# First unit of the attention's maxima moved up: half-head stores, tiles taken in pieces, and two row transfers on ScalarE's queue

## The chip, the cores and the metric

The kernel runs on one core of a Trainium2 chip, as one launch. The metric is the time of one execution on the device, in microseconds (us). The median of three runs of the kernel before is 1208.4 us (1208.12 to 1208.51). One more execution was profiled.

The engines are called as the profile calls them: PE (TensorE; PEld is its weight load), DVE (VectorE), ACT (ScalarE), POOL (GpSimd) and SP (SyncE, which here only issues transfers). ACT issues transfers as well, between its own instructions, and each engine takes its instructions in order.

## What is computed

The input is x of 8 batches by 1024 tokens by 256 columns, in float32. The reference applies half a mixture-of-experts layer, an attention layer with 16 heads of 16 columns, and another half mixture-of-experts layer, each on the layer norm of x and each added to x. An expert that more tokens choose than its capacity allows is dropped whole:

```python
x = x + 0.5 * ffn(layernorm(x), gate_w, w1, b1, w2, b2)
x = x + attn(layernorm(x), Wq, bq, Wkv, bkv, Wo, bo)
x = x + 0.5 * ffn(layernorm(x), gate_w, w1, b1, w2, b2)
...
# attn:  q, k, v = heads of 16 columns;  dots = (q * 16**-0.5) @ k.T, masked above the diagonal
#        out = softmax(dots) @ v;  return out @ Wo.T + bo
# ffn:   top-2 of softmax(x @ gate_w.T); keep = counts <= cap; only kept experts add to the output
```

The kernel computes the attention first as if no expert were kept, counts the choices of both gates on the way, and runs the experts only where one is kept. In the profiled execution that does not happen, so all of the time is the function `attention`.

## The kernel before

**Units.** For each batch b the 16 heads are handled as four units of four heads: unit u = 4 b + g, 32 units in all (NU). A unit has 18 maxima steps (M) and 18 exponent steps (E). An M step (`m_steps`, `fill`) multiplies a piece of q by k on PE into the tile sm, adds the causal mask on PE (masked, before_k), and DVE reduces it to row maxima (mx). After the M steps of one half of the queries, `settle` joins and negates the maxima on DVE (mxr, mneg, mside), and `send` stores them to DRAM (rows) and loads them back as rows (neg) for the next product. An E step (`e_steps`, `fill`) adds neg by a product with take_m and the product of k and q into sc on PE; ACT takes the exponential (pT), POOL zeroes the masked part of diagonal pieces, and a few steps later PE multiplies pT by the values (pav).

**Order.** Every instruction of the attention is issued through a `Lane` (lines 618 to 635), which pins each engine's instructions, and each transfer queue, to the source's order; this is why the profile puts nearly everything on L626, and why groups are told apart by tile. The loop over u runs the E steps of unit u in turns with M steps of the next units; PE fills the turns with pieces from `work` (next batch's transposes pta, projections pq, values pv), at `rate` pieces per gap, one gap for every third step, and DVE with steps from `side`.

**Projections.** `project(b, gp)` makes q and k of eight heads (gp is 0 or 1). Each is split on ACT and POOL into a high and a low part (whole, high, low), so that products of two parts keep float32's accuracy. SP stores each part for all eight heads, one transfer of shape 8x16x512 (256 KB) a time, 16 of them per (b, gp), to the DRAM tile parts; `fetch(u)` loads the four heads of a unit into a qk tile by four transfers.

**The start.** Lines 1206 to 1240 are written out by hand: read x of batch 0 (in pieces of two, two and four tiles of 128 tokens) and of batch 1, transpose the weights (`turning`), normalise (`prepare_first`, `normed`), transpose (`enter`), project the first eight heads by halves of the tokens with a `fetch` of unit 0 after each half, all values of batch 0 (`values_of(0)`), then the statistics and the first four normalised tiles of batch 1 (`prepare(1)`), memsets, and the fetch of unit 1. Then comes the loop, with u = -1 first: the 18 M steps of unit 0, in turns with `project(0, 1)` at a gap every second step. After them the first gate's choice (`gate_first(0)`, small DVE operations such as lc_f, key_f, cand_f) and the bias of the residual (`biased_late(0)`, x_a on POOL) are taken as side steps.

Of the kernel before, what the change touches and what calls it, by code (L numbers as in the profile page):

```python
# [10 lines left out]
F32 = mybir.dt.float32  # L11
# [9 lines left out]
P = 128  # L21
# [8 lines left out]
def macaron_kernel(  # L30
# [98 lines left out]
                base=-(64 * h + k), channel_multiplier=1,  # L129
            )  # L130
    take_m = const.tile([P, P], F32R, name="take_m")
    nc.vector.tensor_copy(take_m, rows.to_broadcast([P, P]))

    wqT = const.tile([P, DC, D], F32, name="wqT")
    wkT = const.tile([P, DC, D], F32, name="wkT")
# [466 lines left out]
    def attention(run_no, src, dst, gate0, logits, tally):  # L602
# [4 lines left out]
        with stack:  # L607
# [76 lines left out]
            def normed(b, jj):  # L684
                mv, ve, rstd = lns[b]
                for j in (2 * jj, 2 * jj + 1):
                    xn = xns[b, j] = norm.tile([P, D], F32, tag="xn", name=f"xn_a{b}_{j}", bufs=4)
                    ln_apply(xn, xbs[b], j, mv, rstd[:, j : j + 1])
                    yield
                if b:  # L690
                    biased(b, jj)

            coming = {}
# [28 lines left out]
            def prepare_first():  # L722
                st, mv = ln_tiles("a0", "a")
                ve = norm.tile([P, TB], F32, tag="vea", name="ve_a0")
                rstd = norm.tile([P, TB], F32, tag="rstda", name="rstd_a0")
                lns[0] = (mv, ve, rstd)
                for n in (slice(0, TB // 2), slice(TB // 2, TB)):
                    for j in range(TB)[n]:
                        ln_stats(xbs[0], j, st, mv)
                    on.gpsimd.tensor_scalar(ve[:, n], mv[:, n, 1], EPS, None, ALU.add)  # L730
                    on.gpsimd.tensor_tensor(rstd[:, n], ve[:, n], half[:, n], ALU.pow)

            def enter(b):
                xnT = xnTs[b] = ap.tile([P, DC, S], F32, tag="xnT", name=f"xnT{b}", bufs=1)
# [19 lines left out]
                    yield True  # L754


            def project(b, gp):
                xnT = xnTs[b]
                parts = parts_d[b, gp] = passing.tile([2, 8, 4, HD, S], F32, tag=f"parts{gp}", name=f"parts{b}_{gp}")
                for s0 in range(0, S, 512):  # L760
                    for t, (wT, bT, scale) in enumerate(((wqT, bqT, QSCALE), (wkT, bkT, 1.0))):
                        pq = bank(f"pq{b}_{gp}_{s0}_{t}")
                        for o in (0, 256):
                            for c in range(DC):
                                product(
                                    pq[:, o : o + 256],
                                    wT[:, c, gp * P : (gp + 1) * P],
                                    xnT[:, c, s0 + o : s0 + o + 256],
                                    start=(c == 0),
                                    stop=(c == DC - 1),  # L770
                                )
# [3 lines left out]
                        high = ap.tile([P, 512], F32R, tag="high", name=f"high{b}_{gp}_{s0}_{t}", bufs=3)  # L775
                        low = ap.tile([P, 512], F32R, tag="low", name=f"low{b}_{gp}_{s0}_{t}", bufs=3)
                        on.scalar.activation(whole, pq, AF.Identity, bias=bT[:, gp : gp + 1], scale=scale)
                        on.scalar.copy(high, whole)
                        on.gpsimd.tensor_tensor(low.bitcast(F32), whole, high.bitcast(F32), ALU.subtract)
                        for c in range(4):  # L780
                            part = (high, low)[c // 2 if t else c % 2]
                            on.sync.dma_start(out=parts[t, :, c, :, s0 : s0 + 512], in_=part.bitcast(F32))
                        yield True


# [62 lines left out]
            def m_steps(u):  # L848
# [56 lines left out]
                def settle(hf):  # L905
                    mx = ap.tile([P, 4, 2, 2], F32, tag="mxr", name=f"mxr{u}_{hf}")
                    on.vector.tensor_reduce(
                        mx.rearrange("p x b a -> p x a b"),
                        mx_tiles[u % 3][hf].rearrange("p h r (a b) s -> p (h r) a b s", a=2),
                        AX.X,  # L910
                        ALU.max,
                    )
                    yield
                    mx = mx.rearrange("p x b a -> p x (b a)")
                    neg = ap.tile([P, 4, 2, 4], F32R, tag="mneg", name=f"mneg{u}_{hf}")
                    high, low = neg[:, :, 0], neg[:, :, 1]
                    on.vector.tensor_scalar(high, mx, -1.0, None, ALU.mult)
                    yield
                    on.vector.scalar_tensor_tensor(
                        low.bitcast(F32), mx, -1.0, high.bitcast(F32), ALU.mult, ALU.subtract  # L920
                    )
                    yield
                    turned = ap.tile([P, 32], F32, tag="mside", name=f"mside{u}_{hf}")
                    on.vector.transpose(turned, neg.bitcast(F32).rearrange("p x c i -> p (x c i)"))
                    start(send(hf, turned), 0)
                    yield

                def send(hf, turned):
                    rows = passing.tile([8, 512], F32, tag="rows", name=f"rows{u}_{hf}")
                    on.sync.dma_start(out=rows.rearrange("c (i s q) -> s c i q", i=4, s=4), in_=turned)  # L930
                    yield 6
                    for h in range(2):
                        on.sync.dma_start(
                            out=negs[u % 2][hf][64 * h : 64 * h + 2, :, :512].bitcast(F32),
                            in_=rows[4 * h : 4 * h + 4].rearrange("(r c) s -> c r s", c=2),
                        )
# [271 lines left out]
            next(turning, None)  # L1208
            next(turning, None)
            drain(read(1))  # L1210
            for t in (vaugs[0], *mx_tiles[0]):
                on.gpsimd.memset(t, 1.0 if t is vaugs[0] else -3.0e38)
            prepare_first()
            for jj in range(2):
                drain(normed(0, jj))
            next(turning, None)
            entering = enter(0)
            next(entering)
            next(entering)
            for jj in range(2, 4):  # L1220
                drain(normed(0, jj))
            projecting = project(0, 0)
            for _ in range(8):
                next(projecting)
            drain(fetch(0, 0, 512))
            drain(entering)
            drain(projecting)
            drain(fetch(0, 512, 512))
            drain(turning)
            drain(values_of(0))  # L1230
            drain(prepare(1))
            for t in (vaugs[1], *mx_tiles[1], *mx_tiles[2]):
                on.gpsimd.memset(t, 1.0 if t is vaugs[1] else -3.0e38)
            for pair_of in negs:
                for t in pair_of:
                    on.gpsimd.memset(t.bitcast(F32), 0.0)
            drain(fetch(1))

            work = deque([project(0, 1)])
            side += [biased_late(0), gate_first(0)]  # L1240
            timed = []
            behind = [0.0]
            last_on = []
# [41 lines left out]
            def maxima():  # L1285
                v, k = divmod(stream[0], 18)
                if v == NU:
                    return
                if k == 0:
                    units[v] = m_steps(v)  # L1290
                steps, settle, done = units[v]
                steps[k]()
                if k == max(done, 8) or k == 17:
                    side.appendleft(settle(int(k == 17)))
                    urgent[0] = 4
                if k == 17:
                    units.pop(v)
                stream[0] += 1

            for u in range(-1, NU):  # L1300
                b, g = divmod(u, NG)
                rate, every = 17 / 12, FILLS
                if u < 0:
                    pass
                elif g == 0:
                    spare[0] = False
                    if b + 1 < B:
# [1 line left out]
                        if b:  # L1309
                            work.append(mixed(leave(b - 1), project(b + 1, 1)))  # L1310
                        else:
                            work.append(project(b + 1, 1))
                        work.append(values_of(b + 1))
                    if b:
                        start(divide(b - 1, 1, 0), 4)
                        after[u - 1, 1] = divide(b - 1, 1, 1)
                        side.append(gate_first(b))
                elif g == 1 and b + 1 == B:
                    work.append(leave(b - 1))
                elif g == 2:  # L1320
                    if b == 0:
                        start(read(2), 40)
# [14 lines left out]
                    start(fetch(u + 2, lag=6), 8)  # L1337
                if u < 0:
                    for n in range(18):
                        step(maxima, 2, 4 if n < 5 else 4 / 3, 1)  # L1340
                else:
                    if u == 0:
                        for n in range(3):
# [86 lines left out]
```

## Time and profile before

| what | us |
|---|---|
| median of three runs | 1208.4 |
| the profiled execution's own time | 1207.5 |
| its span, first to last instruction | 1205.5 |
| busy: PE, DVE, ACT, POOL | 1138.4, 935.2, 735.6, 433.8 |
| first M reduction on DVE starts | 46.16 |
| first exponential (unit 0) starts on ACT | 77.35 |
| first exponential of unit 4, the second batch's first | 220.2 |

Times inside the profile are counted from the first instruction. The page cuts the span in 40 slices of 30 us. A row of a timeline has its start, its length, the engine, the operation, output<-input, shapes and a count, and in brackets the idle time before it and what ended it; a "q" behind an engine means the part of it that issues transfers. In the view by stretches each engine's busy time is followed by its number of instructions, and at the end stand the granted PE clock, the busy share of the 16 DMA engines and the GB/s they moved.

### The profile page before, as it was taken

To read this page: it belongs to the slowest core of one execution; us is meant where nothing else is said; L and a number is where in the kernel's file an instruction comes from. 1 tells how busy PE (TensorE), PEld (TensorE's weight loads), DVE (VectorE), ACT (ScalarE), POOL (GpSimd) and SP (SyncE) were. 2 spreads that over 40 slices of the span, in tenths; PEclk is the share of its full clock that TensorE was granted. 3 is DMA by queue.
4 is the path that set the end of the run, shared out by engine and by line. 5 is a ranking of instruction groups with operands and counts; after the bars stand their busy time and mean duration, and the time that the engine had idled before them with its cause. 6 is when DMAs were issued, how large, how long until landed. Compare 5 with 4: busy or idle time off the path is not lost.

```text
span 1205.5 us, 36314 instructions
## 1 busy us (share of the span) xinstructions
PE 1138.4 (94%) x15178; PEld 663.1 (55%) x15178; DVE 935.2 (78%) x1652; ACT 735.6 (61%) x955; POOL 433.8 (36%) x772
## 2 busy tenths in 40 slices
PE   6789899999999999999999999999999999999983
PEld 4445555655556555655556555565556555555542
DVE  2687558887788877988788877888789888798834
ACT  3236656766666666665666656566666666665671
POOL 4633313543333423532235433333235322232331
PEclk9879999999999999999999999999999999999997
DMA  5644654354554646455563645546564555543211
GB/s 178 222 168 141 209 173 128 111 196 153 171 185 154 198 159 190 143 172 177 157 201 113 207 153 168 169 155 202 160 181 150 176 174 177 155 136 109 63 42 39
DMA packets 108517, 190.25 MB, mean 158 GB/s; under 512 B 24752, under 2 KB 42296, under 8 KB 108344
## 3 DMA queue, kind: packets, MB, share of 16 engines
q1 hardware_dynamic: 104952, 185.59, 47.8%
q8 instruction: 122, 2.00, 0.7%
q10 hardware_dynamic: 3392, 2.24, 0.6%
q14 instruction: 51, 0.42, 0.1%
HBM read 94.50 MB, written 93.31 MB: 156 GB/s over the span
## 4 chain that ended last, share of the span: by engine, by line
PE 76%; DVE 13%; DMA 5%; issue 1%; ACT 1%; POOL 1%; SPq 1%; POOLq 0%; ACTq 0%; DVEq 0%
PE sc L626 22%; PE pav L626 21%; PE sm L626 15%; PE pq L626 8%; DVE mx L626 8%; PE px L626 4%; PE pv L626 4%; PE pta L626 2%; DVE st_a L626 1%; DMA few<-sums 1%; DMA neg<-rows 1%; DMA rows<-mside 1%; SPq L626 1%; DVE mv_a L626 1%; DMA qk<-parts 1%
## 5 line engine op out<-in xcount | busy, mean ns | idle before, releaser
L626 DVE TENSOR_REDUCE mx<-sm 128x2 f32<-128x1024 f32 (+2 forms) x576 | 684.7, 1215 | 161.6 <-PE sm L626 159.9
L626 ACT ACTIVATE pT<-sc 128x1024 f32<-128x1024 f32 x576 | 573.0, 1022 | 309.6 <-PE sc L626 297.9
L626 PE MATMUL pav<-pT,vaug 128*32 128x256 f32 (+3 forms) x4608 | 329.7, 387 | 2.0 <-ACT att L626 1.4
L626 POOL TENSOR_SCALAR_AFFINE_SELECT pT<-pT 128x256 f32<-128x256 f32 (+1 forms) x448 | 191.0, 443 | 297.2 <-ACT pT L626 290.4
L626 PE MATMUL sm<-qk 64*128 64x512 f32 (+3 forms) x1536 | 266.2, 384 | 17.4 <-DVE mx L626 8.4
L626 PE MATMUL sc<-neg,take_m 64*128 64x512 f32 x1152 | 263.7, 454 | 16.6 <-DVE mx L626 8.9
L626 PE MATMUL sc<-qk 64*128 64x512 f32 (+3 forms) x1536 | 228.7, 334 | 0.0
L626 PEld LDWEIGHTS sm<-qk 64*128 64x128 f32 x1536 | 140.7, 187 | 120.4 <-issue 51.9
L626 POOL TENSOR_TENSOR low<-whole,high 128x512 f32<-128x512 f32 x64 | 82.0, 1282 | 311.3 <-ACT high L626 302.5
L626 PEld LDWEIGHTS pav<-pT,vaug 128*32 128x32 f32 x4608 | 113.7, 109 | 108.0 <-issue 52.2
L626 PEld LDWEIGHTS sc<-neg,take_m 64*128 64x128 f32 x1152 | 109.4, 186 | 106.8 <-issue 53.6
L626 PEld LDWEIGHTS sc<-qk 64*128 64x128 f32 x1536 | 146.2, 186 | 16.3
L626 PE MATMUL sm<-masked,before_k 64*128 64x128 bf16 (+1 forms) x1280 | 86.3, 213 | 0.0
L626 PE MATMUL pq<-xnT,wqT 128*32 128x256 f32 x1024 | 76.3, 391 | 0.5 <-ACT xnT L626 0.5
L626 PE MATMUL px<-woT,on 128*32 128x264 f32 x1024 | 76.5, 387 | 0.2 <-ACT on L626 0.2
L626 PE MATMUL pq<-xnT,wkT 128*32 128x256 f32 x1024 | 73.2, 395 | 0.0
L626 PE MATMUL pv<-wvT,xnT 128*32 128x264 f32 x1024 | 72.3, 390 | 0.0
L626 PEld LDWEIGHTS <-before_k 64*128 64x128 bf16 x1280 | 37.9, 96 | 43.1 <-issue 26.6
L626 POOL TENSOR_TENSOR x_a<-x_a,bo_all 128x512 f32<-128x512 f32 x32 | 41.6, 1304 | 28.1 <-DVE xn_a L626 28.1
L626 PEld LDWEIGHTS pq<-xnT,wqT 128*32 128x32 f32 x1024 | 34.0, 112 | 31.8 <-issue 13.9
L626 DVE TENSOR_TENSOR x_a<-px,x_a 128x256 f32<-128x256 f32 x64 | 26.2, 410 | 31.2 <-PE px L626 30.6
L626 PEld LDWEIGHTS px<-woT,on 128*32 128x32 f32 x1024 | 34.7, 110 | 26.6 <-issue 9.8
(131 smaller groups left out, 741.4 us busy)
## 6 DMA issues: line engine op xcount, KB each, us to landing
qk<-parts SPq DMA_DIRECT2D x124, 512.0 KB
parts<-high SPq DMA_DIRECT2D x128, 256.0 KB
parts<-low SPq DMA_DIRECT2D x128, 256.0 KB
sums<-att SPq DMA_DIRECT2D x62, 256.0 KB
out_dram<-x_a SPq DMA_DIRECT2D x16, 512.0 KB
on<-sums SPq DMA_DIRECT2D x30, 256.0 KB
rs<-inv SPq DMA_DIRECT2D x30, 256.0 KB
x_a<-in_L_attn_x_dram SPq DMA_DIRECT2D x13, 512.0 KB
```

The lines of the kernel that those rows point to most:

```text
L626: i = call(*args, **kwargs)
```

## The change

The start is rearranged, and some rules of the first units change with it:

- The tile take_m is made later on DVE, inside `prepare_first`, which now takes statistics of tiles 0 to 1, 2 to 3, then normalises these four, and only then takes the statistics of tiles 4 to 7. POOL's memsets of the first vaug and mx tiles move from before the first rstd operations to between them.
- The first projection stores only the first four heads of each part (transfers of 4x16x512, 128 KB) and keeps the other four heads' stores in a list `later`. Its parts live in buffers of the tag pT (six of them) and no longer in high and low (three each).
- After the second half's fetch of unit 0, the 16 stores of `later` are issued, then the fetch of unit 1, then the statistics of batch 1 and the memsets. The values of batch 0 go from the hand-written start into `work`, ahead of `project(0, 1)`. The M steps of unit 0 have a gap after every step (16/5 pieces for five steps, then 16/13). The first four normalised tiles of batch 1 become side steps.
- Unit 0's maxima of the first half are settled after its fifth M step and no longer after the ninth. Unit 0's row transfers (rows, neg) are issued by ACT and no longer by SP.
- The first gate's choice and the bias of batches 0 and 1 move into the loop's units 0 and 1. In batch 0 the rate is 13/12 pieces a gap, before 17/12, and batch 1's second projection is mixed with its values where before it preceded them.

```diff
@@ prepare_first
-                for n in (slice(0, TB // 2), slice(TB // 2, TB)):
-                    for j in range(TB)[n]:
+                def some(j0, j1):
+                    for j in range(j0, j1):
                         ln_stats(xbs[0], j, st, mv)
...
+                some(0, 2)
+                some(2, 4)
+                drain(normed(0, 0))
+                next(turning, None)
+                drain(normed(0, 1))
+                on.vector.tensor_copy(take_m, rows.to_broadcast([P, P]))
+                on.gpsimd.memset(vaugs[0], 1.0)
+                for t in mx_tiles[0]:
+                    on.gpsimd.memset(t, -3.0e38)
+                some(4, 8)
@@ project
+                first = b == gp == 0
...
+                        if first:
+                            both = ap.tile([P, 2, 512], F32, tag="pT", name=f"split{s0}_{t}", bufs=6)
+                            high, low = both[:, 0].bitcast(F32R), both[:, 1].bitcast(F32R)
...
                             part = (high, low)[c // 2 if t else c % 2]
-                            on.sync.dma_start(out=parts[t, :, c, :, s0 : s0 + 512], in_=part.bitcast(F32))
+                            heads = parts[t, :, c, :, s0 : s0 + 512]
+                            if first:
+                                later.append((heads[4:], part[P // 2 :]))
+                                heads, part = heads[:4], part[: P // 2]
+                            on.sync.dma_start(out=heads, in_=part.bitcast(F32))
@@ settle and send of m_steps
-                    start(send(hf, turned), 0)
+                    start(send(hf, turned), 0 if u else 2)
...
+                    queue = on.sync if u else on.scalar
...
-                    yield 6
+                    yield 6 if u else 4
@@ the hand-written start
-            for t in (vaugs[0], *mx_tiles[0]):
-                on.gpsimd.memset(t, 1.0 if t is vaugs[0] else -3.0e38)
             prepare_first()
-            for jj in range(2):
-                drain(normed(0, jj))
-            next(turning, None)
             entering = enter(0)
...
             drain(fetch(0, 512, 512))
+            for heads, part in later:
+                on.sync.dma_start(out=heads, in_=part.bitcast(F32))
+            drain(fetch(1))
+            preparing = prepare(1)
+            for _ in range(TB + 1):
+                next(preparing)
...
             drain(turning)
-            drain(values_of(0))
-            drain(prepare(1))
...
-            drain(fetch(1))
-            work = deque([project(0, 1)])
-            side += [biased_late(0), gate_first(0)]
+            work = deque([values_of(0), project(0, 1)])
+            side.append(preparing)
@@ the loop
-                if k == max(done, 8) or k == 17:
+                if k == (max(done, 8) if v else done) or k == 17:
...
-                rate, every = 17 / 12, FILLS
+                rate, every = (17 if b else 13) / 12, FILLS
...
-                            work.append(project(b + 1, 1))
-                        work.append(values_of(b + 1))
+                            work.append(mixed(values_of(b + 1), project(b + 1, 1)))
+                        if b:
+                            work.append(values_of(b + 1))
...
-                        step(maxima, 2, 4 if n < 5 else 4 / 3, 1)
+                        step(maxima, 1, 16 / 5 if n < 5 else 16 / 13, 1)
```

In the built program the order of transfers on SP becomes: eight half stores, four loads of unit 0, eight half stores, four loads of unit 0, the 16 half stores of `later`, four loads of unit 1 (512 KB each), the 16 full stores of `project(0, 1)`, and then the first two loads of unit 2. ACT's order is, around its own transfers: rows of unit 0's first half, whole and high of the next part, neg (two transfers), three more pairs of whole and high, rows of the second half, xnT, the first pT, a small exponential of the gate, neg (two transfers), the second pT.

More of the change, by code (lines that the diff above doesn't have):

```diff
@@ L131, in macaron_kernel @@
     take_m = const.tile([P, P], F32R, name="take_m")
-    nc.vector.tensor_copy(take_m, rows.to_broadcast([P, P]))
     wqT = const.tile([P, DC, D], F32, name="wqT")
@@ L689, in normed @@
                     yield
-                if b:
+                if b > 1:
                     biased(b, jj)
@@ L726, in prepare_first @@
                 lns[0] = (mv, ve, rstd)
-                for n in (slice(0, TB // 2), slice(TB // 2, TB)):
-                    for j in range(TB)[n]:
+                def some(j0, j1):
+                    for j in range(j0, j1):
                         ln_stats(xbs[0], j, st, mv)
+                    n = slice(j0, j1)
                     on.gpsimd.tensor_scalar(ve[:, n], mv[:, n, 1], EPS, None, ALU.add)
                     on.gpsimd.tensor_tensor(rstd[:, n], ve[:, n], half[:, n], ALU.pow)
+                some(0, 2)
[8 more added lines that the diff above has]
+                some(4, 8)
             def enter(b):
@@ L754, in enter @@
                     yield True
+            later = []
             def project(b, gp):
+                first = b == gp == 0
                 xnT = xnTs[b]
@@ L774, in project @@
                         whole = ap.tile([P, 512], F32, tag="whole", name=f"whole{b}_{gp}_{s0}_{t}")
-                        high = ap.tile([P, 512], F32R, tag="high", name=f"high{b}_{gp}_{s0}_{t}", bufs=3)
-                        low = ap.tile([P, 512], F32R, tag="low", name=f"low{b}_{gp}_{s0}_{t}", bufs=3)
+                        if first:
+                            both = ap.tile([P, 2, 512], F32, tag="pT", name=f"split{s0}_{t}", bufs=6)
+                            high, low = both[:, 0].bitcast(F32R), both[:, 1].bitcast(F32R)
+                        else:
+                            high = ap.tile([P, 512], F32R, tag="high", name=f"high{b}_{gp}_{s0}_{t}", bufs=3)
+                            low = ap.tile([P, 512], F32R, tag="low", name=f"low{b}_{gp}_{s0}_{t}", bufs=3)
                         on.scalar.activation(whole, pq, AF.Identity, bias=bT[:, gp : gp + 1], scale=scale)
@@ L924, in settle @@
                     on.vector.transpose(turned, neg.bitcast(F32).rearrange("p x c i -> p (x c i)"))
-                    start(send(hf, turned), 0)
+                    start(send(hf, turned), 0 if u else 2)
                     yield
                 def send(hf, turned):
+                    queue = on.sync if u else on.scalar
                     rows = passing.tile([8, 512], F32, tag="rows", name=f"rows{u}_{hf}")
-                    on.sync.dma_start(out=rows.rearrange("c (i s q) -> s c i q", i=4, s=4), in_=turned)
-                    yield 6
+                    queue.dma_start(out=rows.rearrange("c (i s q) -> s c i q", i=4, s=4), in_=turned)
+                    yield 6 if u else 4
                     for h in range(2):
-                        on.sync.dma_start(
+                        queue.dma_start(
                             out=negs[u % 2][hf][64 * h : 64 * h + 2, :, :512].bitcast(F32),
@@ L1219, in attention @@
             next(entering)
-            for jj in range(2, 4):
-                drain(normed(0, jj))
             projecting = project(0, 0)
@@ L1225, in attention @@
             drain(fetch(0, 0, 512))
+            for jj in range(2, 4):
+                drain(normed(0, jj))
             drain(entering)
@@ L1228, in attention @@
             drain(fetch(0, 512, 512))
-            drain(turning)
-            drain(values_of(0))
-            drain(prepare(1))
[L1232 to L1236, printed above, removed]
-            drain(fetch(1))
-            work = deque([project(0, 1)])
-            side += [biased_late(0), gate_first(0)]
+            for heads, part in later:
[4 more added lines that the diff above has]
+                next(preparing)
+            for k in range(2):
+                for t in negs[k]:
+                    on.gpsimd.memset(t.bitcast(F32), 0.0)
+                for t in mx_tiles[k + 1]:
+                    on.gpsimd.memset(t, -3.0e38)
+            on.gpsimd.memset(vaugs[1], 1.0)
+            drain(turning)
+            work = deque([values_of(0), project(0, 1)])
+            side.append(preparing)
             timed = []
@@ L1316, in attention @@
                         after[u - 1, 1] = divide(b - 1, 1, 1)
-                        side.append(gate_first(b))
+                    side.append(gate_first(b))
+                    if not b:
+                        side.append(biased_late(b))
                 elif g == 1 and b + 1 == B:
                     work.append(leave(b - 1))
+                elif g == 1 and b == 0:
+                    side.append(biased_late(1))
                 elif g == 2:
```

## The prediction

> **What bounds the kernel now.** I read the 40 slices first, then the view by stretches (one stretch a unit), then the chain in order of time for the first 140 us, then SP's timeline.
>
> ```profile
> PE   6789899999999999999999999999999999999983
> PEclk9879999999999999999999999999999999999997
> ```
>
> PE is full from the fourth slice on. Only the first 90 us and a place in the fifth slice have room, so the change, which leaves batch 1 and later alone, can win or lose only before unit 4.
>
> ```profile
> 77.30:115.20 37.90, 37.34 (x497) 22.63 (x496) 27.38 (x41) 23.67 (x28) 12.14 (x20) 0.91 0.43 143
> 115.20:156.00 40.80, 35.05 (x456) 20.38 (x452) 22.82 (x26) 23.67 (x28) 12.52 (x22) 0.92 0.60 194
> 156.00:190.10 34.10, 34.10 (x456) 20.02 (x454) 22.73 (x26) 23.50 (x39) 7.85 (x17) 0.99 0.40 132
> 190.10:220.20 30.10, 27.53 (x318) 15.35 (x316) 27.57 (x48) 19.23 (x20) 11.44 (x24) 1.00 0.44 141
> ```
>
> These are units 0 to 3, from first exponential to first exponential. Unit 1 has 5.75 us of idle PE, unit 3, which has no filler left, 2.57.
>
> ```profile
> 42.22 1.68 POOL rstd_a L626
> 43.92 2.33 DVE xn_a L626 x4
> 46.24 1.14 DVE mx L626
> ...
> 67.08 0.92 SPq L626
> 68.09 0.81 SPq L626
> 68.95 1.03 SPq L626
> 70.03 1.22 SPq L626
> 71.36 4.99 DMA neg<-rows
> 76.49 0.84 PE sc L626 x4
> 77.35 1.03 ACT pT L626
> ```
>
> The first reductions wait behind batch 1's normalised tiles on DVE (46.24), and the first exponential behind the rows, which stand on SP's queue behind stores of parts (67.08 to 76.49). Both waits are what the change removes. Next, what SP's queue carries:
>
> ```profile
> 26.84 6.48 SPq L626 DMA_DIRECT2D qk<-parts  x4
> 42.95 9.33 SPq L626 DMA_DIRECT2D qk<-parts  x8
> 143.28 1.19 SPq L626 DMA_DIRECT2D qk<-parts  x1
> ```
> ```profile
> 152.87 0.80 PE L626 MATMUL sm<-qk 64*128 64x512 f32 x2 [5.75 <-issue]
> ```
> ```profile
> 54.00:57.00 3.00, 1.09 (x12) 0.37 (x4) 3.00 (x4) 0.26 (x1) 3.00 (x4) 1.00 1.00 401
> 62.00:66.00 4.00, 2.48 (x16) 0.94 (x16) 4.00 (x6) 0.47 (x1) 1.27 (x1) 0.50 0.53 190
> ```
>
> From 54 to 57 only loads of qk run: all 16 DMA engines busy, 401 GB/s. From 62 to 66 only stores of parts: share 0.53, 190 GB/s, so 262 KB take 1.38 us. In the trace's semaphore updates (my source for every landing below) a load of 128x512 raises its semaphore 16 times, a store of 8x16x512 nine times, rows (4x32x32) five times, neg (2x2x512) three times: one more than the outermost count. So a store uses eight engines. The loads of 26.84 and 42.95 landed by 36.9 and 53.7, the one of 143.28 at 152.78; the last is unit 1's stall.
>
> **The change, part by part.**
>
> *Half stores.* A first-half store is 4x16x512. Not in this trace; the ends are half of 1.38 (0.69 us, still eight engines) and the whole 1.38 (four engines). I take 1.38: the rows transfer, outermost count four, shows four engine updates. Weighed against a rule: the Trainium skill, "DMA: Bandwidth & Descriptors", section "Why a DMA increments its semaphore by 16 and not by 1", says that a transfer of these queues runs on the largest number of engines up to 16 that divides the slowest dimension of both sides, on the lowest-numbered ones. That speaks against this change: four heads mean four engines, and half the bytes take the same time. By the rule the sum is the one below, by halved stores that of the first rival.
>
> *The transfer chain.* ACT can copy xnT at 11.45, when its own transfers are issued (10.39 + 1.04), not 11.86: everything is 0.4 earlier. The first 16 stores and eight loads then take as long as before, so unit 0's second half lands at 53.7 - 0.4 = 53.3. Then come 16 more stores, which before did not exist: 16 x 1.38 = 22.1, to 75.4. Three of unit 1's four loads wait for them. Before, the second load landed 3.0 after the last store (48.8 to 51.8); 512 KB in place of 256 KB adds 0.65, and the next two follow by 1.25 (57.1, 58.4, 59.6 before): 79.0, 80.3, 81.5. Before, unit 1's loads were in at 59.6.
>
> *The maxima.* Unit 0's M steps start when its first loads are in (34.5, before 46.16), but the sixth needs the second half and waits until 48.6 to 52.4; twelve more at 1.2 to 1.5 us end at 67 to 71, before 72.9. That gain is worth nothing by itself: PE's order has unit 1's first three sm (81.5 + 0.8) and a pta (1.1 to 1.9) in front of the first sc.
>
> *ACT in order.* The fourth high of `project(0, 1)` takes the first one's buffer (three buffers) and waits for its second store, the third on SP behind unit 1's loads: 81.5 + 3 x 1.38 = 85.6. Then high 0.6, the issue of rows 0.5, xnT 0.6: first exponential at 87.4, before 77.35. The second stands on ACT behind two neg transfers. These wait for the rows and for the sixth store, whose semaphore one of them shares (81.5 + 6 x 1.38 = 89.8). Rows in SP's queue took 4.94 (66.08 to 71.02), on an idle one 1.96 (92.48 to 94.44). On ACT's own queue, beside stores, they take something between: 88.8 to 91.8. With 0.5 for the issues the second starts at 90.3 to 92.3, before 79.7. Here a rule bears too: the same page, "Issuing engines are not separate DMA queues", says that transfers of ACT and SP interleave on the same 16 engines, so that another issuer saves only issue time. By it the end is 4.9 and not 2.0; since the sixth store holds the issue until 89.8 anyway, that moves the second exponential by 1.5 at most.
>
> PE used part of that wait for pta, which before stood between second and third exponential (3.4 us apart), so the lag shrinks from 11.6: third about 92.9 (83.1), fourth 95.4 (86.1). **First stage: +9 us** (8 to 10.5).
>
> *Units 0 to 3.* PE's work up to unit 4 is the same, so its idle time decides. (a) Unit 1's stall. Before: rows issued at 131.62 with four stores right ahead of them; SP waited for them until 139.27 (7.65), issued four stores (4.0) and the load, which landed 9.5 later: 21.2 in all, needed after 15.4. In the new order two loads stand ahead of the rows: 2.0 to 4.9, say 3.5, then 4.0 and 9.5 make 17.0, needed after 14.5 (13 pieces a unit make it 33 us, not 35). 2 to 2.5 of 5.75 stay: -3.5. (b) The clock was at half from 149.6 to 156.4, with 3.5 us of PE work in it: -1.5 if the shorter stall leaves the clock alone, -0 if not; -1. (c) With filler in unit 3 its 2.57 idle goes: -2.6. (d) The gate's some two dozen DVE operations fall into unit 0, the bias (1.3 us each on POOL) into units 0 and 1. DVE is busy 27.4 of unit 0's 37.9 and POOL 12.1, so both are covered; uncovered, DVE's reductions (1.2 us) set the unit's pace: 0 to +1, say 0.5. (e) The stores of batch 1's second projection spread into units 2 and 3, beside their loads; batches 1 to 7 show idle PE before sm of 0.3 to 1.0 in such places: +0.5.
>
> The take_m copy (0.2), statistics in smaller pieces and the moved memsets cost nothing: xnT waits for ACT's own transfers at 11.45, stats of tiles 4 to 7 end near 13, and their four xn (1.4) are done by 16, while PE reaches them at 17.7. Uncovered, they cost their own 1 to 2 us.
>
> **Sum:** 9 - 3.5 - 1 - 2.6 + 0.5 + 0.5 = +2.9. Against the profiled execution: 1207.5 (span 1205.5 and 2.0 around it) becomes 1210.4; the median lies 0.9 higher, so **1211.3**, 0.24% slower. A measurement of this kernel tells about 0.2% (2.4 us) from no change.
>
> **Rivals.**
> 1. *Half stores take half the time (0.69).* The first eight end about 6 earlier, the second eight 5.5 more, and the 16 late ones take 11: unit 1's loads land at 59. Then M sets the pace: start at 31 (PE's pt_b ends), five steps with eight pv of 0.89 until 42.6, thirteen of 1.2 to 1.5: 58 to 62; first exponential near 65, -11 to -12 for the stage, with units 0 to 3 at -6: **1191**. For it: it is what half the bytes suggest. Against: the counts of updates.
> 2. *Not slower: the loop makes up for the start.* Stores of 1.3 (the spacing of the first eight landings), rows in 2.0, and unit 1's stall gone with its clock loss: +7 - 5.75 - 1.75 - 2.6 = -3: **1205**. For it: the lower rate leaves SP fewer stores around unit 3's loads. It decides when the last of them lands before the unit's last M step.
> 3. *The stall stays in unit 1, whole.* The new order still has four stores right before that load. If SP is held by neg as long as before, (a) and (b) are lost, and one more such wait in units 2 or 3 costs 1 to 2: **1216.5**.
>
> **How the numbers follow.** Forecast 0.42, with its own range 1208 to 1214: slower 0.22, same 0.20. Rival 1: 0.12, faster. Rival 2: 0.22, faster 0.15, same 0.07. Rival 3: 0.24, slower 0.23, same 0.01. Together faster 0.27, same 0.28, slower 0.45. The range 1196 to 1219 holds the forecast, rival 2 and most of rival 3, and leaves out rival 1 and the tail of 3.
>
> **What would show it.** Right: stores of 4x16x512 with five updates and a DMA share near 0.27 from 54 to 75; unit 1's loads landing near 81; PE idle for some ten us before sm<-qk there; first exponential near 87, unit 4's near 223; an idle piece of 2 us before sm<-qk in unit 1. Wrong: a first exponential before 75 (rival 1), unit 4 before 218 (rival 2) or after 226 (rival 3). What I may have missed is a wait in units 0 to 3 that the new order makes, and the clock, which was at half for 6.8 us pieces in the old start and whose pieces I can't place in the new one.

## The result

| | kernel before | changed kernel |
|---|---|---|
| median of six runs of each on one chip | 1207.25 us | 1216.31 us |
| the profiled execution's own time (span) | 1207.5 (1205.5) | 1216.3 (1214.6) |
| first exponential | 77.35 | 86.56 |
| start of units 1, 2, 3 and 4 | 115.2, 156.0, 190.1, 220.2 | 127.5, 163.7, 195.6, 228.7 |
| start of unit 31 | 1150.9 | 1158.0 |

The ratio is 1.0076, with a 95% interval of 1.0059 to 1.0093: the change makes the kernel slower by 0.76%, 9.1 us. The prediction said slower by 0.24%, so the sign is right and the forecast size is a third of the real one. The time lies above the forecast's own range of 1208 to 1214 us.

Two rows of the slices of the changed kernel answer to those shown of before:

```profile
PE   6758999999999999999999999999999999999983
PEclk9778999999999999999999999999999999999997
```

The head has become thinner: the third slice (61 to 91 us) was 8 and is 5. The view by stretches, from first exponential to first exponential of units 0 to 3:

```profile
86.60:127.50 40.90, 34.48 (x456) 20.77 (x452) 29.11 (x48) 22.57 (x29) 12.43 (x21) 0.91 0.49 162
127.50:163.70 36.20, 33.95 (x422) 19.13 (x420) 23.51 (x27) 22.14 (x29) 17.20 (x26) 1.00 0.50 160
163.70:195.60 31.90, 31.90 (x422) 18.61 (x420) 22.74 (x26) 22.87 (x33) 9.07 (x18) 1.00 0.47 148
195.60:228.70 33.10, 32.76 (x420) 18.57 (x420) 28.33 (x49) 22.35 (x29) 12.07 (x21) 1.00 0.56 184
```

PE is idle in them for 6.42, 2.25, 0 and 0.34 us (length less busy time); before it was 0.56, 5.75, 0 and 2.57. Unit 1's idle time has shrunk and unit 3's is nearly gone, as forecast, but unit 0 has 5.9 us of new idle time, as much as both gave. Unit 4 starts 8.5 later than before, where 2.9 was forecast. Batch 1 takes 139.5 us in both, and the rest differs by 0.7, so in these two profiles the loss is made before unit 4.

Where it is made, in the timelines of the changed kernel, first PE, then ACT:

```profile
77.78 0.79 PE L625 MATMUL sm<-qk 64*128 64x512 f32 x2 [10.16 <-DMA qk<-parts]
95.27 1.93 PE L625 MATMUL pta<-ident,xn_a 128*32 128x128 f32 x32 [4.66 <-ACT xnT L625]
```
```profile
85.42 0.62 ACT L625 CAST high<-whole 128x512 fp32r<-128x512 f32 x1 [16.99 <-DMA parts<-high]
85.50 0.54 ACTq L625 DMA_DIRECT2D rows<-mside  x1
...
86.56 1.03 ACT L625 ACTIVATE pT<-sc 128x1024 f32<-128x1024 f32 x1
...
93.13 0.55 ACTq L625 DMA_DIRECT2D neg<-rows  x2
93.72 1.02 ACT L625 ACTIVATE pT<-sc 128x1024 f32<-128x1024 f32 x1 [5.99 <-DMA rows<-mside]
```

ACT stands at the fourth high from 68.4 to 85.4, because its buffer is released by a store queued behind unit 1's loads. DVE had the second half's mside ready at 68.8, but the rows stand behind that high in ACT's order and are issued at 85.50. Then ACT stands at neg until the rows have landed. The second exponential starts 14.0 later than before (93.72 for 79.69), the third and the fourth 12.0 and 12.3.

### The profile page after: what moved, and what is told of

The parts are those of the page before. It is cut to its first block, busy times and chain, and to the rows that moved or that the text cites. A ratio compares the mean times of both kernels' runs of the same rounds, so it can differ in the third digit from the quotient of the medians.

```text
span 1214.6 us, 36325 instructions
## 1 busy us (share of the span) xinstructions
PE 1135.6 (93%) x15178; PEld 661.1 (54%) x15178; DVE 937.8 (77%) x1652; ACT 734.1 (60%) x955; POOL 433.1 (36%) x774
## 4 chain that ended last, share of the span: by engine, by line
PE 78%; DMA 7%; DVE 5%; POOL 3%; ACT 2%; SPq 2%; issue 2%; ACTq 0%; POOLq 0%; DVEq 0%
PE sc L625 23%; PE pav L625 22%; PE sm L625 15%; PE pq L625 8%; PE pv L625 4%; PE px L625 4%; DVE mx L625 3%; SPq L625 2%; DMA parts<-split 2%; PE pta L625 2%; DMA rows<-mside 2%; DMA qk<-parts 1%; DMA neg<-rows 1%; ACT pT L625 1%; DMA parts<-high 1%
## 5 line engine op out<-in xcount | busy, mean ns | idle before, releaser
L625 POOL TENSOR_TENSOR low<-whole,high 128x512 f32<-128x512 f32 x60 | 76.9, 1282 | 302.1 <-ACT high L625 268.7
L625 PE MATMUL sm<-masked,before_k 64*128 64x128 bf16 (+1 forms) x1280 | 86.3, 212 | 0.0
L625 PE MATMUL px<-woT,on 128*32 128x264 f32 x1024 | 75.3, 387 | 0.9 <-ACT on L625 0.9
L625 PE MATMUL pv<-wvT,xnT 128*32 128x264 f32 x1024 | 75.7, 393 | 0.0
L625 PEld LDWEIGHTS px<-woT,on 128*32 128x32 f32 x1024 | 34.7, 110 | 26.6 <-issue 10.4
L625 ACT COPY vaug<-pv 128x256 f32<-128x256 f32 x64 | 24.2, 378 | 40.9 <-PE pv L625 40.9
```

Source lines behind the costliest of these rows:

```text
L625: i = call(*args, **kwargs)
```

## The experiments

Each kernel was measured beside the kernel before on the same chip, and the ratios are to that. "Unit 4" is the time of its first exponential in the profile (before: 220.2). Ratios are of medians, the other columns come from one profiled execution each. A time in brackets is that of the kernel compared with.

| kernel | ratio, 95% interval | first exponential | unit 0 | unit 1 | unit 4 |
|---|---|---|---|---|---|
| the changed kernel | 1.0076, 1.0059 to 1.0093 | 86.6 | 40.9 | 36.2 | 228.7 |
| half_stores_alone | 1.0170, 1.0137 to 1.0203 | 98.9 | 35.4 | 36.7 | 236.1 |
| loop_rate_alone | 0.9934, 0.9909 to 0.9960 | 76.2 | 34.2 | 32.6 | 208.4 |
| full_stores | 1.0020, 0.9996 to 1.0043 | 71.2 | 42.3 | 36.5 | 215.0 |
| rows_on_sp | 1.0131, 1.0109 to 1.0153 | 87.8 | 42.8 | 36.6 | 232.2 |
| neg_later | 1.0118, 1.0090 to 1.0145 | 85.8 | 43.0 | 36.4 | 230.2 |
| fourth_free | 1.0073, 1.0044 to 1.0103 | 85.7 | 34.7 | 36.2 | 221.6 |
| gate_back | 1.0074, 1.0050 to 1.0099 | 86.9 | 38.7 | 33.5 | 224.0 |
| both_free | 1.0021, 1.0004 to 1.0037 | 86.3 | 33.2 | 33.6 | 218.0 |
| full_gate | 0.9972, 0.9951 to 0.9993 | 73.6 | 39.9 | 33.2 | 211.7 |
| full_gate_late | 0.9946, 0.9924 to 0.9968 | 75.3 | 35.8 | 33.4 | 209.4 |
| spread | 0.9971, 0.9950 to 0.9992 | 74.2 | 39.8 | 33.4 | 214.5 |
| fewer_ahead | 0.9866, 0.9842 to 0.9891 | 71.2 | 40.3 | 32.5 | 209.2 |

**The half stores alone, in the kernel before.** The parts of the first projection live in the pT buffers here too, as in the change (that hunk is not shown).

```diff
...
+                            heads = parts[t, :, c, :, s0 : s0 + 512]
+                            if first:
+                                later.append((heads[4:], part[P // 2 :]))
+                                heads, part = heads[:4], part[: P // 2]
...
             drain(fetch(0, 512, 512))
+            for heads, part in later:
+                on.sync.dma_start(out=heads, in_=part.bitcast(F32))
```

> The kernel before with the half-head stores and the late ones alone. If the late stores are the cost: unit 1's loads land near 81 (59.6), the row transfers, which stand on SP behind the stores of the second projection, move with them, first exponential 88 to 98 (77.35), and 1217 to 1228. If they are hidden and the rest of the change costs the 9 us: 1205 to 1209.

1226.22 us, 20 slower than the 1206.38 beside it. PE's timeline has the two waits that the expectation named:

```profile
78.20 0.80 PE L626 MATMUL sm<-qk 64*128 64x512 f32 x2 [11.02 <-DMA qk<-parts]
82.25 0.79 PE L626 MATMUL sm<-qk 64*128 64x512 f32 x2 [2.53 <-DMA qk<-parts]
97.50 0.89 PE L626 MATMUL sc<-neg,take_m 64*128 64x512 f32 x2 [12.46 <-DMA neg<-rows]
```

The first two are unit 1's loads behind the late stores, the third the first half's neg, whose rows SP could issue only at 83.27 (66.08 before). So the late stores cost more alone than the whole change does; the rest of it gives 11 us back.

**The loop's rate alone, in the kernel before.**

```diff
-                rate, every = 17 / 12, FILLS
+                rate, every = (17 if b else 13) / 12, FILLS
...
-                            work.append(project(b + 1, 1))
-                        work.append(values_of(b + 1))
+                            work.append(mixed(values_of(b + 1), project(b + 1, 1)))
+                        if b:
+                            work.append(values_of(b + 1))
```

> The kernel before with the loop's rule alone: 13/12 pieces a gap in batch 0 and batch 1's second projection mixed with its values. By the terms of the prediction (stall of unit 1 down by 3.5, clock 1, unit 3's idle 2.6, stores +0.5): 1200 to 1202. By what units 1 to 3 of the changed kernel's trace show (101.2 us for 105.1): 1203 to 1204.5. If PE's work is only moved between the units and a stall comes back elsewhere: 1206 to 1209.

1197.94, 8 faster than the 1206.38 beside it, more than either estimate. The stretches of its units 0 to 3:

```profile
76.20:110.30 34.10, 33.72 (x463) 20.56 (x461) 24.94 (x37) 22.52 (x26) 11.11 (x19) 0.94 0.40 131
110.30:142.90 32.60, 32.35 (x424) 18.77 (x422) 23.15 (x27) 22.16 (x28) 9.53 (x20) 1.00 0.53 170
142.90:175.40 32.50, 32.47 (x422) 18.57 (x420) 22.44 (x26) 22.75 (x32) 8.77 (x18) 1.00 0.52 162
175.40:208.40 33.00, 32.11 (x412) 18.09 (x412) 28.06 (x49) 22.44 (x29) 12.35 (x22) 1.00 0.53 160
```

They last 132.2 us, before 142.9: 7.3 less idle PE (8.88 to 1.55), and 3.4 less busy time for the same work, since PE's clock is halved for less of it (0.94 and 1.00 in units 0 and 1, before 0.91 and 0.92). Unit 4 starts 11.8 earlier than in the kernel before, of which the median keeps 8.4. In the changed kernel the same four units last 142.1. So with the same loop rule something else adds 10 us to them; the next runs look for it.

**All heads stored at once, in the changed kernel.**

```diff
-                            if first:
-                                later.append((heads[4:], part[P // 2 :]))
-                                heads, part = heads[:4], part[: P // 2]
```

> The changed kernel, but the first projection stores all eight heads at once, so the 16 late stores are gone. If the late stores set the first stage (they ran from 52.9 to 74.4 in the changed kernel, 1.29 us each, and unit 1's loads behind them landed at 75.6 to 81.5): the eight full stores land at the same 1.29 to 1.38 as the half ones, unit 1's loads land near 59, the 10.2 us of idle PE before sm<-qk are gone, the first exponential starts near 70 to 73 (86.6), and the time is 1200 to 1205. If the order of the start and the row transfers on ACT's queue cost the time, and not the late stores: first exponential after 80 and 1211 to 1217.

Unit 1's loads land at 59.1 and the first exponential starts at 71.2, as expected of the late stores. But the time is 1209.25, above the forecast: unit 0 takes 42.3 us, and its largest idle piece is the one of the changed kernel again:

```profile
80.92 1.94 PE L625 MATMUL pta<-ident,xn_a 128*32 128x128 f32 x32 [4.41 <-ACT xnT L625]
```

ACT issued the rows at 70.18; they landed at 75.21, and the two neg transfers could be issued only at 76.52 and 79.09, when the stores that had their semaphores had landed (76.50 and 79.07). The second exponential stands behind them and starts at 79.37.

**neg later on ACT.**

```diff
-                    yield 6 if u else 4
+                    yield 6 if u else (12 if hf else 4)
```

> The changed kernel, with the two neg transfers of unit 0's second half issued on ACT three exponentials later; nothing else. If the wait of ACT on them costs what the trace suggests (from 87.7 to 93.1 ACT stood on rows, which landed 7.61 us after their issue, and PE was idle 4.66 us before a pta): second exponential at 88 to 90 (93.7), PE's idle piece gone, and 1211 to 1214 (1216.3). If PE loses that time elsewhere in unit 0 anyway: 1215 to 1217.

The second exponential starts at 86.85, so ACT no longer stands there. But the time does not fall: 1220.36 is above both forecasts. ACT now stands between the fourth and the fifth exponential (first row, of ACT), and PE waits for neg itself:

```profile
97.22 1.02 ACT L625 ACTIVATE pT<-sc 128x1024 f32<-128x1024 f32 x1 [5.46 <-DMA parts<-high]
98.52 0.76 PE L625 MATMUL sc<-neg,take_m 64*128 64x512 f32 x1 [4.59 <-DMA neg<-rows]
101.01 0.79 PE L625 MATMUL sc<-neg,take_m 64*128 64x512 f32 x1 [1.73 <-DMA neg<-rows]
```

The rows had landed at 91.71. The neg transfers were issued at 94.32 and 96.86, right after two stores of the second projection that had their semaphores (94.30 and 96.84), and landed by 100.97, where the changed kernel has 95.70. So the wait only moved, as the second forecast has it, and grew; the edit made neg itself later. It doesn't tell what made the rows late; the next run does.

**A free buffer for the fourth high.**

```diff
-                        if first:
+                        if first or b == s0 == t == 0 and gp:
-                            both = ap.tile([P, 2, 512], F32, tag="pT", name=f"split{s0}_{t}", bufs=6)
+                            both = ap.tile([P, 2, 512], F32, tag="pT", name=f"split{gp}_{s0}_{t}", bufs=6)
```

> The changed kernel, with the first part of the second projection in a buffer of the tag pT, so that the fourth high finds a free buffer and ACT no longer stands there until 85.4. If that wait holds the rows of the second half, which DVE had ready at 68.8 and ACT issued at 85.5: rows issued near 70 and landed before 80, the neg transfers held only by the sixth store (near 89.4), second exponential near 90 (93.7), first still near 86 (unit 1's loads), 1212 to 1213.5. If only unit 1's loads set the stage and the second exponential is made up for: 1215 to 1217.

The rows are issued at 71.09 and have landed at 75.96 (93.11), the neg transfers are off ACT's way, and the second exponential starts at 87.23. That is earlier than expected, because the semaphores that neg shares now belong to stores that had landed by 84.83. Unit 0 falls from 40.9 to 34.7 us and unit 4 starts 7.1 earlier. So the wait for the buffer did hold the rows. The measured time, though, is 1215.42, not in the 1212 to 1213.5 expected for this case but in the other forecast's range, and its ratio can't be told from the changed kernel's.

**Gate and bias back in the start.**

```diff
-                if b > 1:
+                if b:
                     biased(b, jj)
...
-            side.append(preparing)
+            side += [preparing, biased_late(0), gate_first(0)]
...
-                    side.append(gate_first(b))
-                    if not b:
-                        side.append(biased_late(b))
+                        side.append(gate_first(b))
...
-                elif g == 1 and b == 0:
-                    side.append(biased_late(1))
```

> The changed kernel, with the first gate's choice and the bias of batches 0 and 1 taken back to the 18 M steps of unit 0, where the kernel before has them. If they cost the loop's units what the runs so far suggest (unit 1 took 32.6 us with the loop's rate alone, where they are not in it, and 36.2 in the changed kernel, where POOL has six x_a of 1.29 in it): unit 1 near 33, units 0 to 3 together 3 to 5 shorter, 1211 to 1213.5 (1216.3). By the prediction's +0.5 for them: 1215 to 1217.

Units 0 and 1 last 72.2 us together, for 77.1; unit 4 starts 4.7 earlier, inside the range expected for the trace. The time, 1216.01, does not show it: it lies in the range of the +0.5. What these operations did in the changed kernel stands in its groups of unit 1 (127.5 to 163.7) on POOL, and in its chain of waits between 123 and 131 us, where the bias x_a stands in front of the masking of pT and of low. The last row is PE's, waiting for that masking:

```profile
L625 POOL TENSOR_TENSOR x_a<-x_a,bo_all 128x512 f32<-128x512 f32 x6 | 7.6, 1280 | 0.0
L625 POOL TENSOR_SCALAR_AFFINE_SELECT pT<-pT 128x256 f32<-128x256 f32 (+1 forms) x15 | 6.5, 451 | 10.3 <-ACT pT L625 10.3
```
```profile
123.41 0.70 ACT whole L625
124.16 1.28 POOL x_a L625
125.75 0.41 POOL pT L625
126.15 1.24 POOL low L625
127.39 0.59 POOL pT L625
127.98 2.49 POOL x_a L625 x2
```
```profile
138.87 1.03 PE L625 MATMUL pav<-pT,vaug 128*32 128x192 f32 x11 [0.43 <-POOL pT L625]
```

This is a reading of the trace; no run moves the bias without the gate, so what each of them costs is not split.

**Both of these**, since neither alone was seen in the time.

> The changed kernel with both: gate and bias in the start, and a free buffer for the fourth high. In the profiles the one took 4.7 us off the start of unit 4 (224.0 for 228.7) and the other 7.1 (221.6). If they are separate costs: unit 4 near 217, before the 220.2 of the kernel before, and 1205 to 1209. If both shorten the same idle pieces of unit 0: unit 4 near 220 to 222, and 1211 to 1215.

They nearly add up in the trace: unit 4 at 218.0, units 0 to 3 lasting 131.7, as with the loop's rate alone (132.2). And now the time shows it: 1208.06, ratio 1.0021 for 1.0076, and the intervals don't overlap. Of the 10.7 us in the trace the medians keep 6.6. Unit 4 starts 2.2 us earlier than in the kernel before, though the first exponential is 9.0 later, and yet the time is 0.2% longer. Why each alone moved unit 4 by 4.7 and 7.1 us and not the median is open. The single profiles kept 1.8 and 3.2 us of it at the end of the span; the rest went in batches 2 to 7 and the last unit, by pieces of 1 to 2 us. One trace is no fine measure of that stretch: from unit 4 to the end it lasted 985.9 to 990.8 us in the nine profiles whose code there is the same (the changed kernel, full_stores, rows_on_sp, neg_later, fourth_free, gate_back, both_free, full_gate and full_gate_late).

**The rows back on SP.**

```diff
-                    queue = on.sync if u else on.scalar
+                    queue = on.sync
```

> The changed kernel with unit 0's row transfers back on SP. In SP's order the first rows then stand behind the late stores and unit 1's loads, their neg behind four more stores, the second rows behind all 16 stores of the second projection. If ACT's queue spares them that: first exponential near 90 (86.6), the sixth, which needs the second neg, after 107 (103.1), 1219 to 1224. If ACT's standing on them is the greater cost: second exponential right behind the first, 1211 to 1215.

1221.27, as expected of ACT's queue sparing them something. The first exponential is only 1.3 later (87.8); the wait is where the second half's neg is needed, and the sixth exponential starts at 105.3 (103.1):

```profile
103.94 0.90 PE L625 MATMUL sc<-neg,take_m 64*128 64x512 f32 x2 [6.83 <-DMA neg<-rows]
```

**Versions that join the gains.** Full_gate has the edits of full_stores and gate_back, and full_gate_late that of neg_later too. Spread is full_gate_late with the gate and the bias in unit 2 and not in the start, and fewer_ahead is full_gate_late with fewer pieces between unit 0's M steps:

```diff
@@ spread
-                if b:
+                if b > 1:
                     biased(b, jj)
...
-            side += [preparing, biased_late(0), gate_first(0)]
+            side.append(preparing)
...
                 elif g == 2:
                     if b == 0:
+                        side += [gate_first(0), biased_late(0), biased_late(1)]
@@ fewer_ahead
-                        step(maxima, 1, 16 / 5 if n < 5 else 16 / 13, 1)
+                        step(maxima, 1, 16 / 5 if n < 5 else 12 / 13, 1)
...
-                rate, every = (17 if b else 13) / 12, FILLS
+                rate, every = (17 if b else 14) / 12, FILLS
```

> Both: all eight heads stored at once in the first projection, and gate and bias back in the start. If the two costs are separate they add: what the first took off in its own run (some 7 to 8 us against the changed kernel) and 3 to 5 more, 1203 to 1206. If the gate and the bias are then on the path of the start, because the late stores no longer hide them: 1207 to 1211.

1202.75, just below the range: 12.5 us less than the changed kernel by the ratios, where full_stores alone has 6.8 and gate_back alone 0.2. So the gate's gain shows in the time once the late stores are gone.

> The same, with the neg transfers of unit 0's second half issued by ACT after the fourth exponential and not after the first. With the late stores gone the rows land near 75 and the semaphores that neg shares with stores are free near 79, so ACT should not stand there: second exponential near 74 (79.4 with full stores alone), unit 0 near 37, 1195 to 1200, faster than the kernel before. If PE then waits for neg before the sixth sc as long as ACT did (as it did with the late stores in): 1203 to 1206.

1200.77. Without the late stores the later neg does shorten unit 0 (39.9 to 35.8), but the first exponential comes 1.7 later. The time is between the two forecasts, and its interval overlaps with full_gate's.

> All heads stored at once, the second neg transfers after the fourth exponential, and the first gate's choice and the bias of batches 0 and 1 in unit 2, where DVE is busy 22.7 of 31.9 us and POOL 9.1, instead of in the start or in units 0 and 1. If those operations cost only where DVE or POOL are late: first exponential near 71, units 0 to 3 near 36, 33, 34 and 33, unit 4 near 207, 1193 to 1198, the fastest of all. If they cost the same 4 to 5 us wherever they lie: unit 2 near 36, 1199 to 1203.

1203.10, a miss. Unit 2 is only 0.3 longer for the gate, as the first theory has it, but unit 3 is 1.7 longer, with 20.3 us on POOL. The first exponential starts at 74.2, not near 71, and unit 0 lasts 39.8, 4.0 more than in full_gate_late: the sixth sc waits 3.4 us for neg (1.2 in full_gate_late), and PE's clock is at half for 6.8 us of the unit, in full_gate_late for 3.4. Moving the gate did not pay.

> The version with all heads stored at once, gate and bias in the start and the second neg transfers after the fourth exponential, with fewer pieces of the second projection between the M steps of unit 0 (12/13 a gap for 16/13, and 14/12 for 13/12 in batch 0's units), so that fewer stores are ahead of the rows. In the version without this the rows were issued at 73.4 behind five stores and landed at 79.3, and neg at 87.1. If the stores ahead set the wait for neg: rows landed by 77, neg by 84, unit 0 near 34.5 (35.8), 1196 to 1199. If the pieces left over come back as a longer unit 0 or a late load of unit 2: 1200 to 1205.

1189.90, the fastest of all: 1.34% below the kernel before and 2.1% below the changed kernel. It is below both forecasts, and its reason is not the expected one. The rows landed by 74.68 and neg by 85.42 (87.14), but unit 0 lasts 40.3, longer than without the edit: the first exponential comes 4.2 earlier, and neg only 1.7. First exponential and unit 0 together end where they did, and unit 4 starts at 209.2 for 209.4. In the two profiles the difference, 7.9 us of span, comes after that: batch 1 takes 138.3 for 139.5, batches 2 to 7 up to unit 30 take 758.7 for 764.1, with 4 us less busy time on PE for the same instructions. The two were also measured on different chips, though with the kernel before at 1206.54 and 1206.17 there. No run tells why, so that the version is faster is measured, and the cause is open.

## Why the prediction was right in sign and wrong in size

**Half stores: right.** A store of 4x16x512 raises its semaphore five times and lands mostly 1.24 to 1.30 us after the one before it, no faster than the full one; the 16 late ones last from 52.9 to 74.4, 21.5 us for the 22.1 forecast. The DMA share beside them is the 0.27 announced:

```profile
62.00:66.00 4.00, 4.00 (x60) 1.76 (x52) 4.00 (x5) 1.31 (x2) 1.65 (x2) 1.00 0.28 103
```

So the first rival is out. The rule of the Trainium skill ("DMA: Bandwidth & Descriptors", "Why a DMA increments its semaphore by 16 and not by 1"), that the slowest dimension sets the number of engines, agrees with these counts.

**Transfer chain and first exponential: right.** Unit 1's loads landed at 75.6, 77.6, 79.4 and 81.5 (79.0 to 81.5 forecast), PE stood 10.16 us, the third full store landed at 85.35 (85.6), and the first exponential started at 86.56 (87.4): 9.2 later than before. Half_stores_alone and full_stores show the late stores as the cause.

**ACT in order: the step that failed first.** The forecast let the rows take 2.0 to 4.9 us on ACT's queue and held the second exponential until 90.3 to 92.3; then it had the lag shrink, to 9.8 and 9.3 at the third and fourth. The rows took 7.61 us, outside both ends, since the bounds came from rows with fewer stores in flight, four and none: here six were under way when the rows were issued, and these landed (93.11) after the fifth (92.46), just ahead of the sixth (93.74). And the lag did not shrink: PE needed the xnT that ACT had not copied, and the third and fourth exponential came 12.0 and 12.3 late. In unit 0 this wait is worth 6.2 us (40.9 to 34.7 with a free buffer, which gave neg other semaphores too). The forecast did have the rows behind the fourth high, but took the wait to be covered, by the sixth store that neg needs anyway and by PE's pta. What it did not ask is what it costs that rows ready at 68.8 stand 16.7 us on ACT behind a high that waits for a store. Fourth_free shows it: with the buffer free, the rows are in before the first exponential.

**(d), gate and bias: the term most mis-sized.** It was +0.5, with the average busy shares of DVE and POOL as cover. Taking them out of units 0 and 1 takes 4.9 us off these. POOL was busy for less than half of unit 1, but in the trace its x_a of 1.28 us stand in front of the masking that PE's pav waits for, and of low. A busy share told nothing of that. That the bias and not the gate is the cost is read from the trace only.

**(a), (b), (c): right in kind, too small in sum.** (a) came out as forecast in the changed kernel: unit 1's idle PE fell by 3.5, with 1.18 us left before an sm<-qk whose load landed just before it (161.27). But that is luck in part, since of its terms only the 4.0 for the four stores came out: the rows took 6.6 us (143.10 to 149.72) and not 3.5, the load 7.5 (153.76 to 161.27) and not 9.5, and PE asked for it 17.1 us after the rows' issue and not 14.5. (c) fell by 2.2 of 2.6. The cost (e) does not show: unit 2 has no idle PE. But the loop rule by itself takes 10.7 us off units 0 to 3, where these four terms had 6.6: unit 1's stall goes whole, and the clock gives 3.4 for the 1 of (b). The errors offset each other in part: -10.7 in place of -6.6, and against it the ACT wait and (d), together 10.4 by both_free, in place of 0.5. In the trace units 0 to 3 became 0.8 shorter, not 6.1. So the sign rests on the late first exponential.

**The maxima moved up were "worth nothing by itself": half true.** They don't bring the first exponential before unit 1's loads. But with the late stores in place, the changed kernel reaches it 12.3 earlier than half_stores_alone, where M steps and row transfers are as before. Rows_on_sp places only 1.3 of this on ACT's queue; the rest, which comes with the early M steps and the new order of the start, was not split further.

**The rivals.** The third gave the nearest number (1216.5), but not by its mechanism: it had the stall whole in unit 1 and another in units 2 or 3, and the trace has neither. It also was the one to expect unit 4 after 226, and 228.7 came, for another reason. The second fails by its start (9.2 for 7) and by the gate and ACT, not by the loop, which alone makes up for 10.7 where it asked 10.1.

## What to carry to other kernels

A transfer put off to "later" is still in front of every transfer issued after it: ask what lands behind it. An engine that issues transfers between its own instructions waits there for its data, for the semaphores it shares with other queues' stores, and for whatever stands ahead in its order, so follow an instruction back past the first wait to when its data was ready. And an operation is not covered because its engine is idle half of the time; look at what is queued right behind it, and try each such move alone, since here one part of the change was worth 8 us of gain inside a change that lost 9.

## What was not expected of the hardware

A small transfer on ACT's queue waited for SP's stores. The rows of unit 0's second half (128x32) took 4.1 to 7.6 us there, with two to six of SP's stores under way at their issue; the first half's took 2.0 to 3.0 in the kernels with full stores, where at most one store and one load were under way, and 3.9 to 6.3 in those with late stores, of which SP issued four to seven meanwhile. SP's own rows with nothing else under way took 1.96 (in the kernel before, at 92.48). They did not simply queue up behind all of SP's stores: those issued at 85.50 landed between the fifth and the sixth of six. The Trainium skill ("DMA: Bandwidth & Descriptors", "Issuing engines are not separate DMA queues") says that transfers of all issuers interleave on the same DMA engines and that another issuer only saves issue time. The first agrees. For the second, rows_on_sp shows more: with the rows on SP, where they stand behind loads and stores that SP waits for, the ratio is 1.0131 and not 1.0076. So the other issuer also spared them SP's order, at the price of ACT's own standing.

PE's clock was at half longer where PE was idle longer. The pieces at half that begin before the first exponential add up to 23.9 us in the kernel before, 30.7 in the changed one, 41.0 in half_stores_alone and 13.7 in full_stores, with PE idle for 21.3, 32.3, 45.3 and 19.6 up to there: the same order, but not in proportion. The pieces are 3.4, 6.8, 10.2, 13.7, 17.1 or 30.7 us long, multiples of 3.4, and the Trainium skill ("TensorE: Matmul & The Clock Gate", "Part 1: The HAM clock gate (the "warmup" mystery)") describes windows of about that length. In the experiments the single runs of one kernel were up to about 1% apart, and the longer ones mostly had the lower mean granted clock: full_stores ran in 1202.93 at 0.985 and in 1215.15 at 0.978. It isn't the whole of it, since both_free ran in 1202.76 and in 1210.16 at 0.979. So a trace of one execution can show a gain of 5 us that a median does not.
